# Cross-attention and FFN on one core: when the third group's rows are loaded and normalized

## The chip, the core and the metric

The kernel runs on one core of a Trainium2 chip. The metric is the device time of the core in microseconds; the time given for a kernel is the median of its runs. Before the change it is 786.4 us over three runs (785.81 to 787.71).

## The reference

For each of 16 batch entries with 128 rows of 1024 elements, the reference computes a cross-attention layer and a linear layer, both with a residual:

```python
x = x + xattn(layernorm(x), ctx, ctx)      # Wq, Wk, Wv, Wo with biases
x = x + scale * (x_ei(layernorm(x)) @ W)   # W is 0/1; the last fifth of the inputs is weighted by -4
```

The attention has 32 query heads of 32 elements which share 8 key/value heads. Layernorm has no learned weights: (x - mean) / sqrt(var + 1e-5). What matters here is the first layernorm: each row of x is normalized, then transposed, then multiplied by Wq to give the queries.

## The kernel before

**Tiling.** Two batch entries form a group (GB = 2), so there are eight groups, which the code numbers from 0. The loop at L927 has one step for each group. In a step the attention of that group runs (four quarters: two batch entries by two halves of the heads), and between its pieces everything else is placed: the output projection of the group before, the FFN of older groups, and keys, values and queries of the group after. The text calls them the first step (grp 0), the second step (grp 1) and so on.

**The order is written by a planner.** `Stream` (L23) builds the program when the kernel is traced. It holds a list of generators (`queue`), a list of timed events (`events`) and a planned clock (`now`). `piece` takes the next piece of TensorE work from the list and advances the clock by what the piece yields; `later(us, fn)` puts an event on the list; `run` (L52) emits, before each piece, every event that is due. If the list of pieces is empty while the planned end of the quarter is not yet reached, it fires the earliest event whether due or not, and looks again. The chip never sees this clock: it only fixes the order in which each engine receives its instructions. Every engine then runs its own instructions in that order, each waiting for what it needs.

**Rows of x for the queries.** `load_x` (L166) issues one DMA of 512 KB from SP into a buffer of the tag "turn", of which there are two. For groups from the third on, `get_x` (L887) issues the two loads and plans `rows_x` (L356) for each. `rows_x` puts on VectorE two `bn_stats`, a `bn_aggr` and an add of eps (L283, L287, L289), on GpSimd the power -0.5 (`rs_a`, L291), and on VectorE the subtract-and-multiply that writes `xq` (L292). `through_dram` (L302) then plans a store of `xq` to DRAM from SP 2.5 us later on the planned clock, and 7.0 us later four loads back into a "turn" buffer, in an order of elements that lets VectorE transpose it in blocks (`turn_x`, L366). `turn_rows` (L894) plans those transposes 30 to 36 us into the step.

The second group is prepared otherwise: its rows lie in the two "turn" buffers as well (L852), are normalized in place, and TensorE transposes them in `prep_x` (L340) during the first step. So the third group's rows can be loaded only after these transposes.

**The first step** consists, after `prep_x` of the second group, of `convert_ffn`, which converts the FFN weights on ScalarE, and of the second group's queries, `qs[1]`: seven products after Strassen's scheme (`seven`, L462), each of eight pieces of TensorE work. After the fortieth piece, `residuals` loads the two residual tiles x of the first group and plans eight adds of the bias `bo` to them on GpSimd (L180), four for each tile.

**The second step** begins with the output projection of the first group, `out_proj` (L623), again seven products. Its accumulator `o_u` is used by four of them in turn and read by VectorE between (L676), so a product that adds to `o_u` must wait for VectorE's read of the product before it; `o_v` is used by two products in the same way. Its left operands s1 to s4 are sums that VectorE makes (L644). Weight pieces of 512 KB come through a ring of eight buffers: `fetch` (L220) issues the next load from SP when a piece has been used. Output-projection pieces appear in the profile as `piece<-in_L_xattn_Wo_dram` and `piece<-o`.

**Queues.** All these DMAs are issued by SP in the planned order. An SP instruction that has to wait holds up all DMAs behind it. The same holds on VectorE and on GpSimd for the instructions there.

Of the kernel before, what the change touches and what calls it, by code (L numbers as in the profile page):

```python
# [76 lines left out]
def once(fn, *args):  # L77
    fn(*args)
    yield 0.0
# [3 lines left out]
def kernel(  # L83
# [132 lines left out]
    def want(src):  # L216
        feed.append(src)
        return len(feed) - 1
# [63 lines left out]
    def half_stats(stats, src, k):  # L282
        nc.vector.bn_stats(stats[:, k], src[:, k * HALF : (k + 1) * HALF])  # L283
# [12 lines left out]
    def by_quadrant(row):  # L296
        return row.rearrange("p (k c f) -> p c k f", k=NB, c=NC)

    def by_chunk(row):
        return row.rearrange("p (c k f) -> p c k f", k=NB, c=NC)  # L300
# [16 lines left out]
    def new_stats(name):  # L317
        return small.tile([P, D // HALF, 6], FP, tag="stats", name=f"st_{name}")
# [37 lines left out]
    def rows_x(b):  # L356

        src = xns.pop(b)
        stats = new_stats(f"a{b}")
        for k in range(D // HALF):  # L360
            half_stats(stats, src, k)
        row = work.tile([P, D], FP, tag="row", name=f"xq{b}", bufs=2)
        normalize(by_quadrant(row), by_chunk(src), stats, f"a{b}")
        through_dram(row, f"x{b}", 2.5, 7.0, 7.0, lambda c_t: rows.update({b: c_t}))
# [16 lines left out]
    def prep_x(grp, h):  # L381
        yield from turned(xTs, xns, grp, h, "x")
# [447 lines left out]
    with tc.manual_schedule():  # L830
        stream = Stream()

        at_q = {}
        for k in range(2):
            for o in range(2):
                for r in range(2):
                    at_q[r, o, k] = want(lambda r=r, o=o, k=k: q_block(r, o, k))
        qs, os = {1: prep_q(1)}, {}
        for grp in range(NGRP):
            os[grp] = out_proj(grp)  # L840
            if grp + 2 < NGRP:
                qs[grp + 2] = prep_q(grp + 2)

        for _ in range(RING - 2):
            fetch()
        for j in range(GB):
            load_ctx(GB + j)
        for _ in range(2):
            fetch()
        o_parts = [load_o_part(0)]  # L850
        for j in range(GB):
            load_x(GB + j, "turn")  # L852

        def plain(a):
            return prep_q_plain(a, {(r, k): at_q[r, a, k] for r in range(2) for k in range(2)})

        for j in range(GB):
            for h in range(2):
                turn_ctx(j, h)
            stream.add(prep_v(0, [j]))  # L860
        stream.add(prep_k(0))
        stream.run(0.0, lambda: len(stream.queue) > 1)
        nc.vector.tensor_scalar_mul(bqs, bqT, scale)
        for j in range(GB):
            norm_x(j)

        def sums_of_wo():
            def then():
                o_parts.append(load_o_part(1))

            stream.later(10.0, load_ffn)
            stream.later(8.0, lambda: spread(combine("o", 0, o_parts[0]), 3.3, then))

        stream.add(
            prep_x(0, 0),
            prep_x(0, 1),
            once(sums_of_wo),
            once(prep_ctx, 1, 7.0, 9.0, 11.0, 12.0),
            plain(0),
        )  # L880
        stream.run(0.0, lambda: stream.queue)

        def norms(grp, *us):
            for j in range(GB):
                stream.later(us[j], lambda j=j: norm_x(grp * GB + j))

        def get_x(grp):  # L887

            for j in range(GB if grp < NGRP else 0):
                b = grp * GB + j  # L890
                load_x(b, "turn")
                stream.later((10.0 if grp == 2 else 5.0) + 4.0 * j, lambda b=b: rows_x(b))

        def turn_rows(grp):  # L894
            for n, at in enumerate((30.0, 32.0, 34.0, 36.0)):
                stream.later(at, lambda n=n: turn_x(grp * GB + n // 2, n % 2))

        def get_ctx(grp):
            if grp < NGRP:
                for j in range(GB):  # L900
                    load_ctx(grp * GB + j)

        def residuals(grp):
            for j in range(GB):
                load_residual(grp * GB + j, 1.0 if grp == 0 else 4.0)

        def sums_of_wq(k):
            def then():
                for _ in range(4):
                    fetch()  # L910
                if k == 1:
                    spread(combine("o", 1, o_parts[1]), 3.3)

            part = {(r, o): pieces[at_q[r, o, k]] for r, o in BLOCKS}
            if k == 0:
                spread(combine("q", k, part, nc.vector), 1.5, then)
            else:
                spread(combine("q", k, part), 3.3, then)

        def between(gen, n, fn, *args):  # L920

            for i, us in enumerate(gen):
                yield us
                if i + 1 == n:
                    fn(*args)

        for grp in range(NGRP):  # L927
            b0, b1, nxt = grp * GB, grp * GB + 1, grp + 1
            p0, p1 = b0 - 2, b0 - 1
            first, more = grp == 0, nxt < NGRP  # L930
            last = grp == NGRP - 1
            length = 17.4 if first else 23.2 if grp < NGRP - 2 else 19.2
            if first:
                stream.add(
                    once(norms, nxt, 8.5, 25.0),
                    between(plain(1), 9, sums_of_wq, 0),
                    once(sums_of_wq, 1),
                    prep_k(nxt),
                    once(get_ctx, nxt + 1),
                    prep_v(nxt),  # L940
                    prep_x(nxt, 0),
                    prep_x(nxt, 1),
                    once(convert_ffn),
                    between(qs[nxt], 40, residuals, grp),
                )
            elif more:
                stream.add(
                    *([once(get_x, nxt), once(prep_ctx, nxt, 3.7, 8.0, 13.0, 18.0)] if grp == 1 else []),
                    once(turn_rows, nxt),
                    os[grp - 1],  # L950
                    once(get_ctx, nxt + 1),
                    prep_k(nxt),
                    once(load_residual, b0, 4.0),
                    prep_v(nxt),
                    qs[nxt],
                    once(get_x, nxt + 1),
                    once(prep_ctx, nxt + 1, 2.5, 7.0, 11.0, 16.0),
                )

                if nxt < NGRP - 1:  # L960
                    stream.add(ffn(p0), once(load_residual, b1, 2.0), ffn(p1))
            else:
                stream.add(
                    once(load_residual, p1, 1.0, "ctx"),
                    os[grp - 1],
                    once(load_residual, b0, 4.0, "ctx"),
                    ffn(p0 - 2),
                    once(load_residual, b1, 4.0),
                    ffn(p1 - 2),
                )  # L970
            if not more:
                for q in range(2 * NA):
                    b, a = grp * GB + q % GB, q // GB
                    start = stream.now
                    pts = attend(b, a, 15.0)
                    stream.later(15.0, lambda b=b, a=a, pts=pts: weighted(b, a, pts) or 1.0)
                    stream.run(start + 12.0)
                stream.run(stream.now, lambda: (b, a) not in yTs)
                break
            for q in range(2 * NA):  # L980
                b, a = grp * GB + q % GB, q // GB
                start = stream.now
                pts = attend(b, a, length)
                if q == 2 * NA - 1:
                    stream.run(start + length - 2.0, lambda: stream.queue)
                else:
                    stream.run(start + length - 2.0)
                stream.run(stream.now, lambda: None in pts)
                weighted(b, a, pts)
                stream.now += 1.0  # L990
        stream.add(
            os[NGRP - 1],
            ffn(B - 4),
            mixed(ffn(B - 3), ffn_transpose(B - 2), 10, 2),
            mixed(ffn(B - 2), ffn_transpose(B - 1), 8, 2),
            ffn(B - 1),
        )
        stream.drain()
# [49 lines left out]
```

## Time and profile before

| what | value |
|---|---|
| median of three runs | 786.4 us |
| the profiled execution | 785.56 us |
| its span, first to last instruction | 783.8 us |
| TensorE matmul (PE) busy | 765.3 us |
| VectorE (DVE) busy | 488.7 us |
| ScalarE (ACT) busy | 323.1 us |
| GpSimd (POOL) busy | 114.6 us |
| DMA | 192.42 MB, mean 245 GB/s |
| granted TensorE clock | 1.000 |

The profile page gives busy times of the engines, 40 slices of the span, the chain of work that ended last, and groups of instructions. The timeline view, used most here, lists instructions in order of time on one engine: start, duration, engine, line, operation, the tile written and the tiles read, how many were merged, and in brackets how long the engine sat idle before and what released it. PE is TensorE, SPq is the queue of DMAs that SP issues. In the waits view, "A <- B" means that A waited for B.

### The profile page before, as it was taken

How to read it: one execution, taken by the hardware profiler on the slowest of the kernel's cores; microseconds unless marked ns; L12 is line 12 of the kernel's file. 1: busy time of each engine (PE TensorE's matmuls, PEld its weight loads, DVE VectorE, ACT ScalarE, POOL GpSimd, SP SyncE). 2: the span in 40 equal slices, each digit the busy share in tenths (PEclk: the TensorE clock that was granted, in tenths of full speed). 3: DMA queues.
4: the chain of work that ended last, by engine and by line, in shares of the span. 5: the costliest groups of instructions: out<-in, count | busy, mean ns of one | idle time of the engine just before them, and what ended most of it. 6: DMA issues, size and time to landing. Idle time of an engine off the chain costs nothing.

```text
span 783.8 us, 13740 instructions
## 1 busy us (share of the span) xinstructions
PE 765.3 (98%) x5008; PEld 570.7 (73%) x5008; DVE 488.7 (62%) x887; ACT 323.1 (41%) x1261; POOL 114.6 (15%) x142
## 2 busy tenths in 40 slices
PE   5999999999999999999999999999999999999997
PEld 4877884689747986479855898558985689456476
DVE  1358648756766667466784667755676666765552
ACT  0244854435234453344433444344434445575100
POOL 4066502010100102020020200202001010103000
PEclk9999999999999999999999999999999999999999
DMA  9999899969698777878688795977769667763702
GB/s 241 317 332 316 327 342 372 271 196 304 236 299 237 235 237 233 293 215 262 222 270 264 192 290 207 307 230 206 265 216 313 207 199 235 253 202 103 264 27 81
DMA packets 99412, 192.42 MB, mean 245 GB/s; under 512 B 8256, under 2 KB 57728, under 8 KB 99344
## 3 DMA queue, kind: packets, MB, share of 16 engines
q1 hardware_dynamic: 97568, 189.30, 75.4%
q10 hardware_dynamic: 1248, 1.11, 0.6%
q0 software_dynamic: 528, 1.12, 0.6%
q8 instruction: 40, 0.66, 0.4%
q14 instruction: 28, 0.23, 0.1%
HBM read 161.09 MB, written 30.41 MB: 244 GB/s over the span
## 4 chain that ended last, share of the span: by engine, by line
PE 87%; DMA 6%; DVE 4%; POOL 1%; issue 1%; SPq 0%; ACT 0%; DVEq 0%; POOLq 0%
PE f L323 14%; PE o_u L662 13%; PE q_u L451 13%; PE o_v L662 7%; PE tpp L601 7%; PE q_v L451 7%; PE v L323 6%; PE k L323 5%; PE sc L568 4%; PE av L611 4%; PE q_c L451 3%; PE o_c L662 3%; DMA ctx<-in_ctx_dram 2%; DMA wo<-in_L_xattn_Wo_dram 1%; DMA piece<-in_L_xattn_Wq_dram 1%; POOL wo L796 1%
## 5 line engine op out<-in xcount | busy, mean ns | idle before, releaser
L584 ACT ACTIVATE p<-sc,negm 128x128 f32<-128x128 f32 x512 | 181.4, 369 | 133.2 <-DVE negm L580 73.1
L603 ACT COPY pt<-tpp 128x512 f32<-128x512 f32 x128 | 74.7, 591 | 146.8 <-PE tpp L601 146.5
L580 DVE TENSOR_REDUCE negm<-sc 128x4 f32<-128x512 f32 x128 | 86.8, 680 | 45.6 <-PE sc L568 45.6
L584 ACT ACTIVATION_READ_ACCUMULATOR p<-sc,negm 128x1 f32 x512 | 105.5, 206 | 0.0
L323 PE MATMUL f<-wf_sb,x2l 128*128 128x512 f32 x256 | 104.3, 407 | 0.0
L323 PE MATMUL f<-wf_sb,x2h 128*128 128x512 f32 x256 | 100.5, 393 | 0.0
L596 DVE TENSOR_TENSOR p<-p,inv 128x512 f32<-128x512 f32 x128 | 91.9, 718 | 4.4
L451 PE MATMUL q_u<-t,piece 128*128 128x128 f32 x672 | 81.3, 275 | 0.0
L601 PEld LDWEIGHTS tpp<-ident,p 128*128 128x128 f32 x512 | 61.9, 141 | 24.6 <-issue 16.7
L601 PE MATMUL tpp<-ident,p 128*128 128x128 f32 x512 | 75.9, 273 | 3.4 <-DVE p L596 3.2
L451 PEld LDWEIGHTS q_u<-t,piece 128*128 128x128 f32 x672 | 78.1, 192 | 0.1
L180 POOL TENSOR_TENSOR x<-x,bo_b 128x256 f32<-128x256 f32 x64 | 54.3, 874 | 154.7 <-DMA x<-in_x_dram 154.7
L323 PE MATMUL v<-wv_sb,cT 128*128 128x256 f32 x256 | 61.2, 388 | 9.5 <-DMA wv_sb<-in_L_xattn_Wv_dram 7.7
L662 PE MATMUL o_v<-piece,s 128*128 128x512 f32 x128 | 60.3, 598 | 0.5 <-DVE x L676 0.5
L662 PE MATMUL o_u<-piece,s 128*128 128x512 f32 x128 | 59.2, 594 | 0.6 <-DVE x L676 0.6
L323 PEld LDWEIGHTS v<-wv_sb,cT 128*128 128x128 f32 x256 | 47.8, 194 | 16.2 <-DVE cT L349 9.2
L662 PE MATMUL o_u<-piece,yT 128*128 128x512 f32 x128 | 58.6, 600 | 0.0
L323 PE MATMUL k<-cT,wk_sb 128*128 128x256 f32 x256 | 58.0, 380 | 0.0
L323 PEld LDWEIGHTS f<-wf_sb,x2l 128*128 128x128 f32 x256 | 48.2, 188 | 10.5 <-issue 1.1
L323 PEld LDWEIGHTS f<-wf_sb,x2h 128*128 128x128 f32 x256 | 48.2, 188 | 9.6 <-issue 0.5
L323 PEld LDWEIGHTS k<-cT,wk_sb 128*128 128x128 f32 x256 | 47.9, 190 | 8.8 <-issue 2.6
L568 PEld LDWEIGHTS sc<-kT,qT 32*128 32x128 f32 x1024 | 31.4, 186 | 25.7 <-issue 25.7
(86 smaller groups left out, 938.1 us busy)
## 6 DMA issues: line engine op xcount, KB each, us to landing
piece<-o SPq DMA_DIRECT2D x64, 512.0 KB, 4.6
piece<-q SPq DMA_DIRECT2D x56, 512.0 KB, 5.1
piece<-in_L_xattn_Wq_dram SPq DMA_DIRECT2D x50, 512.0 KB, 5.0
piece<-in_L_xattn_Wo_dram SPq DMA_DIRECT2D x48, 512.0 KB, 4.7
xn<-in_x_dram SPq DMA_DIRECT2D x16, 512.0 KB, 6.8
x<-in_x_dram SPq DMA_DIRECT2D x16, 512.0 KB, 5.1
ctx<-in_ctx_dram SPq DMA_DIRECT2D x60, 128.0 KB, 6.7
out_dram<-x SPq DMA_DIRECT2D x15, 512.0 KB, 2.7
```

Source lines behind the costliest of these rows:

```text
L180: lambda cut=cut: nc.gpsimd.tensor_add(x_t[:, cut], x_t[:, cut], bo_b[:, cut]) and None,
L323: nc.tensor.matmul(mm, lhsT=lhsT, rhs=rhs, start=k == 0, stop=k == n - 1)
L451: nc.tensor.matmul(mm if part is None else mm[:, part], lhsT=lhsT, rhs=rhs, start=start and n == k == 0, stop=k == len(some) - 1, skip_gro ...
L568: nc.tensor.matmul(tiles[i][:, g], lhsT=qT[rows, g], rhs=kT[rows, a, cols], start=True, stop=True,)
L580: nc.vector.tensor_reduce(negm, tile_, AX.X, ALU.max, negate=True)
L584: nc.scalar.activation(p[:, g], tile_[:, g], AF.Exp, bias=negm[:, g : g + 1], accum_out=total[:, g : g + 1],)
L596: nc.vector.tensor_mul(p, p, inv.unsqueeze(2).to_broadcast([P, NG, S]))
L601: nc.tensor.transpose(tp[:, g], p[:, g], ident)
L603: nc.scalar.copy(pt, tp)
L611: nc.tensor.matmul(mm[i * HD : (i + 1) * HD], lhsT=vs[b][:, h * HD : (h + 1) * HD], rhs=pts[i], start=True, stop=True,)
L662: nc.tensor.matmul(mm, lhsT=lhsT[:, 2 * k + c], rhs=w[:, c], start=start and k == c == 0, stop=k == c == 1, skip_group_check=True,)
L796: engine.tensor_tensor(dst[:, cols], left[:, cols], right[:, cols], op)
```

## The change

```diff
@@ get_x (L887)
             for j in range(GB if grp < NGRP else 0):
                 b = grp * GB + j
                 load_x(b, "turn")
-                stream.later((10.0 if grp == 2 else 5.0) + 4.0 * j, lambda b=b: rows_x(b))
+                stream.later((24.0 if grp == 2 else 5.0) + (6.0 if grp == 2 else 4.0) * j, lambda b=b: rows_x(b))
@@ the first step (L934)
                     prep_x(nxt, 0),
                     prep_x(nxt, 1),
+                    once(get_x, nxt + 1),
                     once(convert_ffn),
                     between(qs[nxt], 40, residuals, grp),
@@ the other steps (L947)
-                    *([once(get_x, nxt), once(prep_ctx, nxt, 3.7, 8.0, 13.0, 18.0)] if grp == 1 else []),
+                    *([once(prep_ctx, nxt, 3.7, 8.0, 13.0, 18.0)] if grp == 1 else []),
                     once(turn_rows, nxt),
                     os[grp - 1],
```

`get_x(2)`, which loads the rows of batch entries 4 and 5 and plans their normalization, is called in the first step, right after the TensorE transposes of the second group's rows, instead of at the start of the second step. The two `rows_x` are planned 24 and 30 us after the call instead of 10 and 14 us. All other groups keep their times, and `turn_rows` of the third group stays where it is.

## The prediction

> **What bounds the kernel.** I read the page's busy times first, then the waits view for PE, then the timeline of PE in the second step and, as a yardstick, in the third.
>
> ```profile
> PE 765.3 (98%) x5008; PEld 570.7 (73%) x5008; DVE 488.7 (62%) x887; ACT 323.1 (41%) x1261; POOL 114.6 (15%) x142
> ```
>
> PE is the bound: 18.5 us of the span are idle, 9.5 of them in the first 15 us. A change can gain only where PE stalls. Second step:
>
> ```profile
> 118.65 3.70 PE L662 MATMUL o_u<-piece,yT 128*128 128x512 f32 x8
> 125.62 3.60 PE L662 MATMUL o_u<-piece,s 128*128 128x512 f32 x8
> ...
> 134.11 1.98 PE L662 MATMUL o_u<-piece,s 128*128 128x512 f32 x4 [0.58 <-DVE x L676]
> ...
> 139.22 1.98 PE L662 MATMUL o_v<-piece,s 128*128 128x512 f32 x4 [0.53 <-DVE x L676]
> ```
>
> and third step, the same work without a stall:
>
> ```profile
> 214.09 3.70 PE L662 MATMUL o_u<-piece,yT 128*128 128x512 f32 x8
> ...
> 237.02 1.98 PE L662 MATMUL o_v<-piece,s 128*128 128x512 f32 x4
> ```
>
> From the first o_u to the last half of o_v the third step takes 237.02 - 214.09 = 22.93 us; the second takes 143.23 - 118.65 = 24.58 us (143.23 is the start of the same product there). **The loss is 1.65 us**: the brackets hold 1.11, refilling PE after each stall the rest. It splits into 0.75 by the third product (134.11 - 118.65 = 15.46 against 14.71) and 0.90 after it. Its cause on VectorE:
>
> ```profile
> 130.26 1.28 DVE L283 BATCH_NORM_STATS2 st_a<-xn 128x6 f32<-128x512 f32 x2
> ...
> 132.64 0.81 DVE L292 TENSOR_SCALAR xq<-xn,mv_a,rs_a 128x1024 f32<-128x1024 f32 x1 [0.66 <-POOL rs_a L291]
> 133.37 0.68 DVE L676 TENSOR_TENSOR x<-o_u,x 128x512 f32<-128x512 f32 x1
> ```
>
> The read of o_u, which PE needs, stands behind 133.37 - 130.26 = 3.11 us of row work (stats 1.28, mean and eps 0.4, power on POOL 0.66, xq 0.73); the second row does the same before the read at 138.48. No later PE stall of over 0.2 us shows. So **removing both is worth at most 1.65 us, 0.21%**. A measurement of this kernel can tell about 0.3% (2.36 us) from no change, so a gain big enough to be seen is all but excluded.
>
> **Loads moved.** `get_x` now comes at the end of the transposes, which PE finishes at 84.0; SP is behind that point, issuing four pieces from 85.90 on, so the buffers are free and SP doesn't wait. The two loads cost two issues (1.20 us in their old place) and 1 MB, at about 400 GB/s 2.6 us of DMA. Behind them: `piece<-q` fetches, the first used at 103.2 on PE and landing about 96; 7 us of slack. DMA has a hole at 100 to 103 (56 GB/s in one microsecond of it), which takes up the 2.6 us before the residual loads at 108.24. Cost 0; without the hole the residual loads, and all that hangs on them below, come up to 2.6 us later.
>
> **Row 4 moved.** Planned 24 us after the call, it comes before the seventh of the eight pieces of the sixth query product. On DVE it stands before the read at 110.99, behind a free 1.09 us. It runs 109.8 to 112.9, delays that read by 1.9 and the last `p` of the quarter from 111.80 to about 113.7, ending 114.4; its transpose is at 115.24 on PE. POOL is idle there (last work at 90.1). Cost 0, with 0.8 us to spare.
>
> **Row 5 moved: the wait that comes back.** It is planned 30 us after the call. From the call to the end of the first step the planned clock advances by 56 pieces of 0.427, eight transposes of 0.45, one 1.0 and one 1.2: 29.69 us. So it comes after the last query read, before anything of the second step. But POOL has by then been given the eight bias adds (planned from 4 us after the fortieth piece):
>
> ```profile
> 115.63 0.73 POOL L180 TENSOR_TENSOR x<-x,bo_b 128x256 f32<-128x256 f32 x1 [25.55 <-DMA x<-in_x_dram]
> 117.01 5.73 POOL L180 TENSOR_TENSOR x<-x,bo_b 128x256 f32<-128x256 f32 x7 [0.65 <-DMA x<-in_x_dram]
> ```
>
> `rs_a` for row 5 stands behind them. DVE has its mean and eps ready at 117.7 (query read 115.44 + 0.61, then 1.65 of stats), and would wait. The Trainium skill ("PSUM — Partial Sum Buffer", section "Engine vs sequencer instructions") says that the queues of ScalarE, VectorE and GpSimd are strict FIFO; it speaks against this change, and this trace has a row for it:
>
> ```profile
> 166.25 1.21 DVE L292 TENSOR_SCALAR x2n<-x,mv_f,rs_f 128x1024 f32<-128x1024 f32 x1 [5.16 <-POOL rs_f L291]
> ```
>
> There an `rs_f`, ready at 161.1, ran at 165.66, after an add that waited for its residual load. If POOL took what is ready, xq5 would start at 118.4 and the full 1.65 would be won. By row and rule it runs after 117.01 + seven adds of 0.72 (their median) to 0.82 (5.73/7): 122.05 to 122.74; with the power's 0.55 and 0.05, xq5 starts at 122.65 to 123.35.
>
> Queued behind xq5 on DVE: the scores' maximum at 118.73, s1, s2, another maximum, the read of o_u. Before:
>
> ```profile
> 119.34 1.00 DVE L644 TENSOR_TENSOR s<-yT,yT 128x512 f32<-128x512 f32 x1
> 120.38 1.10 DVE L644 TENSOR_TENSOR s<-s,yT 128x512 f32<-128x512 f32 x1
> ...
> 122.44 0.69 DVE L676 TENSOR_TENSOR x<-o_u,x 128x512 f32<-128x512 f32 x1 [0.36 <-POOL x L180]
> ```
>
> After: xq5 frees DVE 0.73 later (123.4 to 124.1), then 0.61 + 0.61 + 0.65 + 0.61, and the read runs from 125.9 to 126.6 and ends 0.65 later. I take the sums at 0.6 (the later s rows take 0.69, 0.6 from start to start), since the adds beside them are over. Second rule, "SBUF — State Buffer", section "Who interferes with whom": a VectorE operation with two SBUF inputs and a GpSimd one that reads SBUF hold one port pair in turn, the loser blocked for the whole instruction. By that each sum could have lost an add of 0.72; the rows lost 0.3 and 0.4, and I take the rows (0.8 us recovered rather than 1.4).
>
> PE wants to add to o_u at 125.62 and gets it at 126.6 to 127.25, with refill **1.15 to 1.85 us late**. Then the old stalls are gone: from that read to the read of o_u at the third product DVE has 133.37 - 122.44 - 3.11 = 7.82 us of work, so it ends at 134.4 to 135.1, where PE arrives at 118.65 + 14.71 + 1.15 to 1.85 = 134.5 to 135.2. **Sum: +1.15 to +1.85 for one new stall, -1.65 for the two old: -0.5 to +0.2 us; I take -0.2.**
>
> **SP.** The planned quarter ends at 29.72 (its start, 14.32, plus 17.4 - 2.0), 0.03 after the pieces do. With no piece left, `run` fires all events: the load-back of row 4, the store of row 5, its load-back. All stand ahead of the fetches of the third product, which SP issued from 120.66. Row 4's store at 113.05 lands after about 8.8 (`piece<-o` at 113.21): 121.9; four issues, 1.75: 123.6. Row 5's store at about 123.9, landing 3.5 (3.7 at 133.48): 127.4; four issues: 129.2. The fetch lands 4.4 later (like that at 129.2): 133.6; PE wants it at 134.5. Slack 0.9 us, cost 0 by these values. Bounds: with landings of 7.7 and issues of 3.23, both seen in this step, 121.9 + 3.2 + 7.7 + 3.2 + 4.4 = 140.4, 6 us late; from below, 0.
>
> **Rivals.**
> - *SP is late, not DVE* (slower): the fetch behind the stores and load-backs decides. For it: four landings in a row on one queue, 0.9 us of slack. Against: with SP blocked DMA runs empty, and landings are then short. It decides from a landing at 134.5. With row 5's store half way between its two landings (3.7 and 7.7, so 5.7) and four issues at 2.6, the fetch lands at 121.9 + 2.6 + 5.7 + 2.6 + 4.4 = 137.2, 2.7 late, and the sum is +2.5: 788.9 us.
> - *Clean gain*: POOL doesn't hold up row 5, since the residuals land earlier or the power goes first. Against it the 5.16 us row. -1.65: 784.8 us.
> - *Late residuals*: the moved loads push the residual loads and the bias adds by 1 to 2.6 us, all of which reaches PE by the new stall: +0.8 to +2.4, about 788.0 us. Against it the hole at 100 to 103.
>
> **Numbers.** The sum is made on the profiled execution (785.56 us, of which the span is 783.8); that lies 0.84 under the median, a difference I take as run to run, so 786.4 - 0.2 = 786.2. Chances: forecast 0.52, SP 0.27, clean gain 0.09, late residuals 0.12. Seen as slower (above 788.8): some 0.18 of the SP case and 0.04 of the late residuals, 0.22. Faster by 2.36: 0.03, only if the yardstick of 1.65 is wrong. The rest, 0.75, is no change. Range 784.8 (clean gain) to 789.6 (a good part of SP's bound); the forecast's own is 785.7 to 787.0.
>
> **To be seen after.** Right: no bracket at the third product and at o_v; a wait of about 5 us at xq on POOL near 118 to 123; a PE bracket of about 1 us near 126 on DVE. SP: a PE bracket on a DMA of `piece<-o` near 134, and no SP issue between 124 and 127. Wrong altogether if row 5 shows a wait of 0.7 us, or if PE stalls before 118.

## The result

The changed kernel takes 788.81 us (median of 22 runs, 785.58 to 790.07), the kernel before 787.12 us (22 runs in the same comparison, 785.72 to 789.5). The ratio is 1.0021 with a 95% interval of 1.0012 to 1.0029: **slower by about 1.7 us (0.9 to 2.3)**. It is less than the 2.36 us counted as a visible change, and inside the range, but the forecast was -0.2. A part of it may be TensorE's clock, which differs from run to run whichever the kernel: among runs with a mean granted clock of at least 0.999 the medians are 787.0 (6 of the 22 runs) and 786.3 (32 of 74 runs of the kernel before, made with the experiments below), among those at 0.997 or 0.998 they are 789.1 and 787.6. At like clock I estimate a loss of 0.7 to 1.5 us from these, though the runs were made at different times.

The spans of the two profiled executions, 788.3 and 783.8 us, lie 4.5 us apart. Not all of it belongs to the change. The last transposes of the second group's rows, after which the two programs first differ, start at 82.94 us before and at 84.81 after: 1.87 us stem from the stretch ahead, whose program both share. Nearly all of it is the clock: from 60 to 64 us the granted clock is 0.57 on average in this execution of the changed kernel and 1.00 in that of the kernel before, which is worth 0.43 x 4 = 1.7 us. So I count from events of the same execution: from the first o_u of the second step to the last half of o_v. Before, the last half of o_v stood here:

```profile
143.23 1.99 PE L662 MATMUL o_v<-piece,s 128*128 128x512 f32 x4
```

That was 24.58 us, and 22.93 in the third step, which has no stall. After the change it is 147.70 - 120.50 = 27.20 us: +2.62. The two numbers, 1.87 and 2.62, are the whole difference of the spans.

The timeline of PE in the second step, changed kernel (start, duration, instruction, in brackets the idle time before it and what ended it):

```profile
120.50 3.70 PE L662 MATMUL o_u<-piece,yT 128*128 128x512 f32 x8
124.04 3.60 PE L662 MATMUL o_c<-piece,yT 128*128 128x512 f32 x8
129.85 3.70 PE L662 MATMUL o_u<-piece,s 128*128 128x512 f32 x8 [2.22 <-DVE x L676]
...
139.41 1.96 PE L662 MATMUL o_u<-piece,s 128*128 128x512 f32 x4 [1.54 <-DMA piece<-o]
...
147.70 1.98 PE L662 MATMUL o_v<-piece,s 128*128 128x512 f32 x4
```

The two old brackets, both of them on VectorE's reads, are gone. Two new ones stand there: 2.22 us before the second product into o_u, and 1.54 us on a DMA at the third. The first on VectorE and GpSimd, same kernel:

```profile
119.45 0.15 DVE L289 TENSOR_SCALAR ve_a<-mv_a 128x1 f32<-128x1 f32 x1
125.86 0.81 DVE L292 TENSOR_SCALAR xq<-xn,mv_a,rs_a 128x1024 f32<-128x1024 f32 x1 [6.26 <-POOL rs_a L291]
```

```profile
119.15 0.72 POOL L180 TENSOR_TENSOR x<-x,bo_b 128x256 f32<-128x256 f32 x1 [5.15 <-DMA x<-in_x_dram]
120.50 4.82 POOL L180 TENSOR_TENSOR x<-x,bo_b 128x256 f32<-128x256 f32 x7 [0.63 <-DMA x<-in_x_dram]
125.28 0.55 POOL L291 TENSOR_TENSOR rs_a<-ve_a,minus_half 128x1 f32<-128x1 f32 x1
```

The power of row 5 could start at 119.6 and starts at 125.28, after all eight bias adds, as foreseen. The second wait on the queue of SP:

```profile
115.09 0.32 SPq L314 DMA_DIRECT2D dram_x<-xq  x1
116.52 1.67 SPq L225 DMA_DIRECT2D piece<-o  x2
125.75 1.74 SPq L311 DMA_DIRECT2D turn_x<-dram_x  x4
127.59 0.38 SPq L314 DMA_DIRECT2D dram_x<-xq  x1
131.81 1.73 SPq L311 DMA_DIRECT2D turn_x<-dram_x  x4
133.64 0.86 SPq L225 DMA_DIRECT2D piece<-o  x2
```

Read it from above. Row 4 is stored at 115.09. Its load-back waits for that store to land, until 125.75, and SP issues nothing in between after 118.2. Then come the store of row 5, its landing at 131.8, its load-back, and only then the fetch of the third product's first piece. That fetch was issued 2.0 us after the first o_u in the kernel before (120.66 against 118.65), and 13.1 us after it now. The kernel before, at the same place:

```profile
120.66 2.04 SPq L225 DMA_DIRECT2D piece<-o  x2
```

### The profile page after: what moved, and what is told of

The parts are those of the page before. It is cut to its first block, busy times and chain, and to the rows that moved or that the text cites. A ratio compares the mean times of both kernels' runs of the same rounds, so it can differ in the third digit from the quotient of the medians.

```text
span 788.3 us, 13739 instructions
## 1 busy us (share of the span) xinstructions
PE 767.9 (97%) x5008; PEld 571.9 (73%) x5008; DVE 486.8 (62%) x887; ACT 322.6 (41%) x1261; POOL 112.8 (14%) x142
## 4 chain that ended last, share of the span: by engine, by line
PE 87%; DMA 6%; DVE 2%; POOL 2%; issue 1%; SPq 1%; ACT 0%; DVEq 0%; POOLq 0%
PE f L323 14%; PE o_u L662 13%; PE q_u L451 12%; PE tpp L601 7%; PE o_v L662 7%; PE v L323 7%; PE q_v L451 6%; PE k L323 6%; PE sc L568 4%; PE av L611 4%; PE q_c L451 3%; PE o_c L662 3%; DMA ctx<-in_ctx_dram 2%; DMA wo<-in_L_xattn_Wo_dram 1%; DMA x<-in_x_dram 1%; POOL wo L796 1%
## 5 line engine op out<-in xcount | busy, mean ns | idle before, releaser
L601 PEld LDWEIGHTS tpp<-ident,p 128*128 128x128 f32 x512 | 62.1, 141 | 24.7 <-issue 16.7
L180 POOL TENSOR_TENSOR x<-x,bo_b 128x256 f32<-128x256 f32 x64 | 52.7, 849 | 129.9 <-DMA x<-in_x_dram 129.9
L323 PEld LDWEIGHTS f<-wf_sb,x2l 128*128 128x128 f32 x256 | 48.2, 188 | 10.6 <-issue 1.1
```

The costliest lines, as they stand in the source:

```text
L180: lambda cut=cut: nc.gpsimd.tensor_add(x_t[:, cut], x_t[:, cut], bo_b[:, cut]) and None,
L323: nc.tensor.matmul(mm, lhsT=lhsT, rhs=rhs, start=k == 0, stop=k == n - 1)
L601: nc.tensor.transpose(tp[:, g], p[:, g], ident)
```

## The experiments

There are two new waits in a row, so it is open which of them costs the time: the later can swallow the earlier. Theory SP says that the piece of the third product comes last and sets the end. Theory POOL says that the wait for the power does. A third, late residuals, says that the moved loads delay the residual loads and with them the adds. The first four kernels are the two edits apart and together, and the loads alone.

**Power ahead of the bias adds.** Only the planned time of the adds changes:

```diff
-    def load_residual(b, us=4.0, tag="x"):
+    def load_residual(b, us=4.0, tag="x", at=4.0):
...
-                4.0 + us * k,
+                at + us * k,
...
-                load_residual(grp * GB + j, 1.0 if grp == 0 else 4.0)
+                load_residual(grp * GB + j, 1.0 if grp == 0 else 4.0, at=9.5 if grp == 0 else 4.0)
```

> The changed kernel, with the eight bias adds of the first group's residuals planned 9.5 us instead of 4 us after their loads, so that GpSimd receives the power of row 5 ahead of them. Theory SP (the weights of the third product are last: their fetches stand behind row 4's load-back, row 5's store and row 5's load-back): the wait of xq5 falls from 6.26 to about 0.7 us and the 2.2 us PE wait near the second o_u product goes, but the fetch lands when it did, so that the wait at the third product grows from 1.5 to about 3.9 us and the last o_v half stays about 27.2 us after the first o_u: time within 0.5 us of the changed kernel. Theory POOL (the wait for the power is the loss): that distance falls by 2.4 to about 24.8 us and the time by as much.

Measured: 789.51 us, ratio to the kernel before 1.0037 (1.0022 to 1.0051). The timeline of VectorE, then of PE:

```profile
118.99 1.21 DVE L292 TENSOR_SCALAR xq<-xn,mv_a,rs_a 128x1024 f32<-128x1024 f32 x1 [0.66 <-POOL rs_a L291]
```

```profile
119.22 3.70 PE L662 MATMUL o_u<-piece,yT 128*128 128x512 f32 x8
...
126.19 3.60 PE L662 MATMUL o_u<-piece,s 128*128 128x512 f32 x8
...
137.08 3.62 PE L662 MATMUL o_u<-piece,s 128*128 128x512 f32 x4 [2.99 <-DMA piece<-o]
...
147.04 1.98 PE L662 MATMUL o_v<-piece,s 128*128 128x512 f32 x4
```

The wait for the power is down to 0.66 us, the second product follows without a bracket, and nothing is won: the third product waits 2.99 us instead, and the last half of o_v comes 27.82 us after the first o_u. 27.2 was expected, but a part of the 27.82 is TensorE's clock: the first half of the third product takes 3.62 us here instead of some 1.9, because the granted clock was 0.50 from 137.0 to 140.4 us in this execution. At full clock I estimate the distance at 26.1 us: the first half took 3.90 us from its start to the second half's, with the transposes between, and 2.22 in the changed kernel, 1.7 less. The half clock begins as PE's wait of 2.99 us ends and may have come with it (see the last section); all six runs of this kernel have a mean granted clock of 0.998 or less. Theory POOL expected 24.8 and falls as the account of the changed kernel also at 26.1, which is what a second profile of the changed kernel shows below (26.12): the wait for the power was hidden behind SP's.

**Nothing fired early.** The planned end of the quarter is moved by 0.1 us, so that the clock has passed it when the pieces run out:

```diff
-                    stream.run(start + length - 2.0, lambda: stream.queue)
+                    stream.run(start + length - (2.1 if first else 2.0), lambda: stream.queue)
```

> The changed kernel, with the planned end of the first step's last quarter 0.1 us earlier, so that no event is fired before its due time: only row 4's load-back still stands ahead of the third product's fetches, row 5's store comes after them, its load-back four fetches later. Theory SP: no PE wait at the third product, the wait of about 2.4 us before the second o_u product stays: last o_v half about 25.3 us after the first o_u, 1.9 us less than the changed kernel. Theory POOL expects the same wait of 2.4 and no more than 0.5 us of gain from SP's order.

Measured: 787.09 us, ratio 1.0005 (0.9996 to 1.0014). On SP the fetch now follows row 4's load-back at once, and on PE one bracket is left:

```profile
122.68 1.74 SPq L311 DMA_DIRECT2D turn_x<-dram_x  x4
124.52 0.85 SPq L225 DMA_DIRECT2D piece<-o  x2
125.47 0.38 SPq L314 DMA_DIRECT2D dram_x<-xq  x1
```

```profile
118.70 3.70 PE L662 MATMUL o_u<-piece,yT 128*128 128x512 f32 x8
...
127.14 3.70 PE L662 MATMUL o_u<-piece,s 128*128 128x512 f32 x8 [1.30 <-DVE x L676]
...
143.28 1.98 PE L662 MATMUL o_v<-piece,s 128*128 128x512 f32 x4
```

The distance is 24.58 us, to the hundredth that of the kernel before, and the time can't be told from it either. The wait before the second product is 1.30 us here, 2.22 in the changed kernel; the expected 25.3 took it over unchanged. So an order of instructions fixed by 0.03 us on a clock that the chip never sees is worth 2.62 us against the first profile of the changed kernel, 1.54 against the second one below, and some 1.3 us by the two ratios (1.0021 and 1.0005).

**Both edits.** The two diffs above together.

> Both edits together: power of row 5 ahead of the bias adds, and nothing fired early. Theory SP with POOL behind it: no PE wait over 0.3 us in the second step's output projection, last o_v half about 22.9 us after the first o_u, 1.65 us faster than the kernel before and about 4.2 us faster than the changed kernel in the profile. Theory late residuals (the moved loads delay the residual loads, and so the adds): the read of the first o_u waits for the adds, and a PE wait of 0.5 us or more stays before the second o_u product.

Measured: 785.13 us, ratio 0.9977 (0.9968 to 0.9986), **1.8 us faster than the kernel before**, whose median beside it was 787.1. PE's timeline has no bracket in the output projection:

```profile
120.19 3.70 PE L662 MATMUL o_u<-piece,yT 128*128 128x512 f32 x8
...
134.91 1.88 PE L662 MATMUL o_u<-piece,s 128*128 128x512 f32 x4
...
143.13 1.98 PE L662 MATMUL o_v<-piece,s 128*128 128x512 f32 x4
```

The distance is 22.94 us, that of the third step. The adds run after the power here, 8 in 7.39 us from 119.90 on, and are done when PE needs the read. (The two edits were not run without the move. That the old stalls stay as long as the row work stays in the second step, the next kernel shows.)

**The loads alone.** From the kernel before: the two loads go out where the change puts them, the row work stays in the second step.

```diff
-                load_x(b, "turn")
+                if grp != 2:
+                    load_x(b, "turn")
...
+                    once(lambda: [load_x(2 * GB + j, "turn") for j in range(GB)]),
                     once(convert_ffn),
```

> The kernel before, with only the two loads of the third group's rows moved to the end of the second group's transposes; the row work stays where it was. Theory late residuals: the residual loads land 8.9 us or more after issue instead of 7.3 to 8.0, and the bias adds start about 1.7 us later against the first o_u (1.35 us ahead of it instead of 3.0). Theory chance (landings differ from execution to execution): they land as before, within 0.5 us. Both expect the time of the kernel before within 0.5 us, as the adds have 2 us to spare there.

Measured: 787.02 us, ratio 0.9999 (0.9991 to 1.0007); the old brackets of 0.58 and 0.54 are back and the distance is 24.58. The windows view shows where the megabyte went (window, its length, busy times of the engines, clock, DMA share, GB/s), first before, then with the loads moved, whose execution runs 1.5 us later:

```profile
100.00:104.00 4.00, 4.00 (x60) 3.88 (x57) 1.28 (x2) 2.92 (x10) 0.00 (x0) 1.00 0.63 160
```

```profile
101.50:105.50 4.00, 4.00 (x59) 3.88 (x56) 1.25 (x2) 2.96 (x10) 0.00 (x0) 1.00 1.08 370
```

(370 - 160) GB/s in 4 us is 0.84 MB: the hole takes most of it, as the prediction had it. The first bias add started 8.45 us after its load's issue, between what the two theories expected.

**A second profile of each kernel** asks whether that is the change or chance.

> The kernel before, looked at once more, for the residual loads. Theory late residuals: the first bias add starts 7.4 us after its load's issue, within 0.4, and 3.0 us before the first o_u, as in the first profile; in the kernels with moved loads it was 8.2 to 9.2. Theory chance: it lies anywhere between 7 and 9.5.

> The changed kernel, looked at once more, for the size of its two waits. Theory late residuals: the first bias add starts 8.2 us or more after its load's issue. Theory SP: whatever the wait before the second o_u product is here (1 to 2.5 us), the third product's start follows the landing of its piece, 5.5 to 5.8 us after the fetch's issue, and the last o_v half lies 1.5 to 3 us later against the first o_u than in the kernel before.

Measured: 788.17 and 791.64 us, one run each, so that only the profiles count. At the first add both came as late residuals had said: it started 7.1 us after its load's issue in the kernel before (7.4 in the first profile) and 8.5 us after it in the changed kernel. With the loads moved it was 8.2 to 9.0 us in all four profiles in which GpSimd had nothing else to wait for and no store stood ahead of those loads. So the moved loads seem to delay the first residual tile, by 0.8 to 1.9 us from its issue (four profiles against two). But what row 5's power waits for is the end of the adds, and the second add needs the other tile. In the kernel before:

```profile
117.80 0.73 POOL L180 TENSOR_TENSOR x<-x,bo_b 128x256 f32<-128x256 f32 x1 [25.39 <-DMA x<-in_x_dram]
120.66 5.73 POOL L180 TENSOR_TENSOR x<-x,bo_b 128x256 f32<-128x256 f32 x7 [2.13 <-ACT yT L619]
```

The second add started nearly three microseconds after the first, and the seven ended at 126.39, 5.4 us after the first o_u (120.98 here). Against the first o_u that end lies at 4.1 and 5.4 us in the two profiles of the kernel before, 4.7 with the loads moved, 4.8 and 4.0 in the two of the changed kernel, 3.9 with nothing fired early. The spread within one kernel is as wide as between them. **That the delay reaches the end of the adds, and so PE, is not shown**; a shift of some tenths can't be excluded.

The second profile of the changed kernel:

```profile
123.16 3.70 PE L662 MATMUL o_u<-piece,yT 128*128 128x512 f32 x8
...
131.74 3.70 PE L662 MATMUL o_u<-piece,s 128*128 128x512 f32 x8 [1.45 <-DVE x L676]
...
140.99 1.95 PE L662 MATMUL o_u<-piece,s 128*128 128x512 f32 x4 [1.24 <-DVE cT L349]
...
149.28 1.98 PE L662 MATMUL o_v<-piece,s 128*128 128x512 f32 x4
```

The distance is 149.28 - 123.16 = 26.12 us, 1.54 over the kernel before: close to the 1.7 of the medians. The name in the second bracket misleads. PE doesn't need that cT here; it needs the piece, which was issued at 135.81 and took 5.0 us to land, to 140.8. (5.5 to 5.8 us had been expected for it.)

**Rows earlier.** To the changed kernel, one number in `get_x`, so that both powers stand ahead of the adds and row 5's store in row 4's old place:

```diff
-                stream.later((24.0 if grp == 2 else 5.0) + (6.0 if grp == 2 else 4.0) * j, lambda b=b: rows_x(b))
+                stream.later((18.0 if grp == 2 else 5.0) + (6.0 if grp == 2 else 4.0) * j, lambda b=b: rows_x(b))
```

> The changed kernel with the two rows' work planned 18 and 24 us after the loads instead of 24 and 30, nothing else. Both powers then stand ahead of the bias adds on GpSimd, and row 5's store goes out where row 4's did, about 5.5 us before the first o_u; only its load-back is fired early and stands ahead of the third product's fetches. Theory SP with POOL: the fetch is issued after that store's landing (about 10 us) and four issues (1.75), 6.3 us after the first o_u instead of 13.1, and lands about 12 after, before the 14.7 at which PE wants it: no PE wait at the third product or before the second, last o_v half near 22.9 us after the first o_u, 1.5 to 2 us faster than the kernel before. If four landings on SP are what counts and not their place, row 4's load-back, now ahead of the second product's last fetches, brings a PE wait on a DMA at the second or third product instead.

Measured: 787.21 us, ratio 1.0001 (0.9990 to 1.0011), and not the gain expected. The second step did as expected, 22.93 us from 121.02 to 143.95 without a bracket. (Row 5's store went out 1.2 us before the first o_u, not 5.5, behind the landing of row 4's. The fetch landed 14.0 us after the first o_u, where about 12 was expected, and was still in time for 14.7.) The price is in the first step:

```profile
109.31 0.63 PE L601 MATMUL tpp<-ident,p 128*128 128x128 f32 x4 [0.48 <-ACT p L584]
...
117.58 0.63 PE L601 MATMUL tpp<-ident,p 128*128 128x128 f32 x4 [0.96 <-DVE p L596]
```

Transposes of the attention wait for `p`, which is late by the row work now ahead of it on VectorE. From the last transposes of the second group's rows (83.51) to the first o_u (121.02) it takes 37.51 us, before 118.65 - 82.94 = 35.71: 1.80 us lost, 1.65 won.

**Load-backs late.** To the kernel with both edits, load-backs planned 27 us after the row work:

```diff
-        through_dram(row, f"x{b}", 2.5, 7.0, 7.0, lambda c_t: rows.update({b: c_t}))
+        through_dram(row, f"x{b}", 2.5, *((27.0, 27.0) if b // GB == 2 else (7.0, 7.0)), lambda c_t: rows.update({b: c_t}))
```

> The kernel with both edits, and the load-backs of both rows planned 27 us after the row work instead of 7, so that none of them stands ahead of the third product's fetches. Theory SP: no wait was left in the second step's output projection, so the time is that of the kernel with both edits within 0.5 us, and the last o_v half stays at 22.9 us after the first o_u. If row 4's load-back still costs something there, it is faster by that.

Measured: 785.21 us, ratio 0.9969 (0.9958 to 0.9980), distance 22.93. The median lies 0.08 us from that of both edits. The kernel before ran slower beside it, 787.51, so that by the ratios it wins 0.6 us more, but the two intervals overlap and the distance is the same: that something was left to win there is not shown.

| kernel | PE waits before the 2nd / at the 3rd product into o_u, us | o_u to last o_v half, us | ratio to before |
|---|---|---|---|
| before | none / 0.58 | 24.58 | 1 |
| changed | 2.22 / 1.54, second profile 1.45 / 1.24 | 27.20, second profile 26.12 | 1.0021 (1.0012 to 1.0029) |
| power first | none / 2.99 | 27.82, at full clock about 26.1 | 1.0037 (1.0022 to 1.0051) |
| nothing early | 1.30 / none | 24.58 | 1.0005 (0.9996 to 1.0014) |
| both | none / none | 22.94 | 0.9977 (0.9968 to 0.9986) |

## Why the prediction was wrong

**What bounds it, and the most to be won: right.** 1.65 us was the bound; with all new waits taken away the profile shows 1.64 (24.58 - 22.94), and the runs 1.8 (1.1 to 2.5). ("No later PE stall of over 0.2 us" overlooked one of 0.42 us on `p` at 719.20, far from the row work; the bound doesn't rest on it.)

**Loads and row 4: right.** The loads cost nothing measurable. Row 4 ran behind its free microsecond, and PE had no bracket in the first step after the transposes.

**Row 5 behind the adds: the mechanism right, the size right in two of three profiles.** Foreseen were a start of xq5 4.0 to 4.7 us after the first o_u and a lateness of 1.15 to 1.85 at the second product. Measured were 125.86 - 120.50 = 5.36 and 129.85 - 120.50 - 6.97 = 2.38 in the first profile, 1.61 (131.74 - 123.16 - 6.97) in the second, and 127.14 - 118.70 - 6.97 = 1.47 with nothing fired early. That last kernel is the forecast's own case, DVE without SP. It came out as the sum had it: between -0.5 and +0.2, at 0.0.

**SP: the step that failed.** The prediction found that all events are fired early and what then stands ahead of the fetch, and wrote "Slack 0.9 us, cost 0 by these values". The values were the fault:

| term of the step | predicted, us | changed kernel, two profiles, us | the row it was read from, second profile of the kernel before, us |
|---|---|---|---|
| landing of row 4's store | 8.8 | 10.6, 9.8 | 10.2 |
| landing of row 5's store | 3.5 | 4.2, 4.8 | 4.1 |
| landing of the fetch | 4.4 | 5.6, 5.0 | 5.8 |
| four issues of a load-back | 1.75 | 1.74, 1.75 | 1.88 |

The three landings together are 2.9 to 3.7 us longer than taken, against a slack of 0.9. Each was read from one row of one execution. The last column has the same three rows in the other profile of the kernel before: together some 20 us there, 17.0 in the first profile and 16.7 as taken. So the spread between two executions of an unchanged kernel is already more than the slack. What makes a landing longer in one execution than in another is open. Three terms in a chain, each read short, decided a case whose slack was below their spread.

An argument on the same step failed too. Against the rival it said that with SP blocked DMA runs empty and landings are then short. SP issued nothing after 118.2, yet the DMA share was 1.03 from there to 124.0, at 405 GB/s: what had been issued lasted nearly until row 4's store landed at 125.7. The third product came 18.91 - 14.71 = 4.20 us late in the first profile and 3.12 in the second, where the forecast had 1.15 to 1.85. So the rival "SP is late", at 0.27, was the case that came, with its sign, a PE bracket on a DMA of `piece<-o`; its price was +2.5; the two profiles show +2.62 and +1.54, the medians +1.7.

A wait that lies after another on the path decides, and takes away what the other would cost: with the power first, time didn't fall.

## What to carry to other kernels

A step moved in the plan takes its stores and load-backs along, and on a queue that waits in order these stand ahead of every fetch behind them: add up store, landing, issue and landing with the spread of each over more than one execution, and where the slack is smaller than the spread, forecast the loss. Look for the engine whose small instruction (here a power of 128 elements) lands behind work that waits for a DMA. And where two waits follow each other on the path, take each away alone and both together; one edit alone would have condemned a change that wins 1.8 us with two small repairs.

## What the hardware showed besides

A store of 512 KB to DRAM, row 4's, landed 8.7 to 10.6 us after its issue while DMA was full, with a share of 0.96 to 1.03 in between (seven executions: 10.6, 9.8, 9.9, 9.6, 10.0, 9.9, 8.7). Row 5's landed 4.2 to 4.8 us after its issue when SP had issued only a load-back since its long wait (three executions).

VectorE's s1 and s2 took 1.00 and 1.10 us beside GpSimd's adds and 0.68 and 0.69 after them. Taken one by one, the instructions show the two engines in turn. In the kernel before an add ran from 119.07. s1 started at 119.34 and took 1.00 us; the add behind, from 119.75, took 1.18 where the others take 0.72; s2, from 120.38, took 1.10; the add from 120.89 took 1.17. With both edits the subtract-and-multiply of xq took 1.21 us beside the adds, 0.81 alone, and the add behind it 1.18. Each loses 0.3 to 0.5 us, which fits a wait for what is left of the other's instruction: s1 had 0.4 us to wait from its start to 119.75. So the prediction's second rule and the 0.3 and 0.4 us that it took from the rows don't contradict each other. The averages hide it, since most adds meet nothing: 0.82 us (5.73 / 7) with VectorE at work, 0.69 (4.82 / 7) with VectorE waiting.

The granted TensorE clock was 0.50 for 3.4 us in one stretch of six of the ten profiles, and a matmul of the output projection that takes 0.59 us took 1.06 in it. In each of the six the stretch begins within 1.1 us of the end of an idle stretch of PE of 2.3 to 3.1 us: near 60 us in five, at 137.0 with power first. Other idle stretches of 2.2 to 2.5 us went without. So a stall that long can cost up to 1.7 us beyond its own length; what decides between the two cases, these traces don't show.
